# Seven products for the first image's keys, earlier loads, and a gate chain and norms that sit elsewhere

## The chip, the cores and the metric

The kernel runs on one core of a Trainium2 chip. The metric is the device time in microseconds (us) of one execution; the time of a kernel is the median of several runs. A profiled execution gives, beside its own time, a span: from its first to its last instruction.

## The reference

The input x is [4, 512, 32, 32]: four images of 512 channels and 1024 tokens. Four layers each add something to x, computed from a group norm of x (32 groups of 16 channels):

```
x = x + L0(gn(x)); x = x + L1(gn(x)); x = x + L2(gn(x)); x = x + L3(gn(x))

L0: q, k, v = w_q xf, w_k xf, w_v xf            # 8 heads of 64
    attn = softmax(w_head mixed over heads (q^T k * scale))
    attn = instance norm over (q, T) of each head; out = (attn v) w_proj^T + b_proj
L1: y = mean of x over the tokens; two layers of RY rotations and CNOTs on 9 qubits,
    q_out = expectations; x * sigmoid(q_out fc_w^T + fc_b)
L2: softmax attention, 8 heads of 64, with Wq, Wkv, Wp
L3: softmax over the 8 best of 2048 memory rows, their weighted sum
```

Everything is float32.

## The kernel before

`fast_net` (line 42) writes the whole order of work out by hand: Python generators are advanced at chosen places, and instructions that go through `pin` (line 56) keep their program order on their engine.

Start. `first` (305) loads x and w_q of image 0, normalizes, and makes q. `circuit` (815) prepares constants: the loads of whp (824, 32 small DMAs on SP), wmix (828), angles, their sine and cosine (854, on ACT), the matrices `turn` of the circuit, turned by fourteen calls of `rotate` (804: three DVE instructions each, lines 807, 808, 811), parities on POOL, and the `signs` (896 to 900). Then `take_k` (452) makes k of image 0 by `project` (193): four blocks of eight matmuls of 128x512 each, copied out by DVE (457). A matmul of float32 appears as two records on PE.

Layer 0 runs image by image in 32 steps of 32 queries (loop at 1721, `step` at 1611). In step s, `scores` (499) makes the scores of step s (510) in PSUM pairs, ACT copies them to ss (516), and eight DMAs, four issued by SP and four by POOL, relay them to s2 (525) so that heads lie side by side; `mix` (532) of step s-2 mixes heads by wmix (536), ACT takes the exponentials (543), DVE turns them (549) and takes their statistics (564), and `apply` (566, line 575) multiplies with v of step s-7. `sums` (583) and `scale` (637) normalize on POOL. In steps 0 to 6 `take_v` (461) makes v in bank pt. After step 31 seven steps follow without scores, in the first four of which q of the next image is made (`take_q`).

Around that, each step advances side work: `mid` (1689) advances `prepare` (423, the norm of the next image) in steps 9 to 12, 24, 28, 30 and 31, and one link of `state["behind"]`; `early` (1684) issues loads from a plan between the two halves of a step's scores. For the next image the plan of `next_image` (270) loads halves of a quarter of x (256 KB, 2 KB rows) in steps 20, 22, 24 and 26, two each in steps 28 and 29, and the four columns of w_q (256 KB, 512 B rows) in steps 30 to 33; they go through ACT's queue (`beside`, 266). For images 1 to 3 `collect` (655) loads further pieces in steps 7 to 18.

k of images 1 to 3 is made by `seven_keys` (1134): `seven` (1086) forms the 2x2 block product from seven products instead of eight (line 1112), each of four matmuls in one PSUM pair, which ACT copies (1145, where a block begins) or DVE adds (1041) to the block. `sums_k` (1116) makes their input sums on DVE: four sets ahead of the products, three more between them. In image 3's tail, k and v of layer 2 are made in the same way (`seven_by_channels` 1242, `seven_v` 1255).

The gate of layer 1 (`gating`, 904) is a chain of about sixteen links for each image, advanced by `next(state["behind"])`: two group averages (152, 162) and their small steps on POOL; `turned(0)` (929) and its rotation on POOL (922 to 926); `turned(1)` (934, 935) and its rotation; pr (939); the products of signs (944); zr (950, 955); the gate's product (959); exponential on ACT (967), reciprocal on DVE (971), and nine steps on POOL (975 to 983). All small products go to bank pt through `small_ps` (60). The chain advances in each of the seven closing steps of an image, then once after each of the seven products, and the rest in the next image's first steps. For `by_scalar` (after layer 0) the small copies run on ACT.

Layer 2 walks units of four key blocks (`scores2` 1340, `apply2` 1381). Between images a border makes q, k and v by seven products each (loops from 1874); `finish2` (1444, line 1452) scales a finished unit on DVE, which frees its PSUM bank; `small_ps` (1809) takes that bank at the border. `norm3` (1477) of the image before, or the gate of image 3 at the first border, is advanced once after each product. In image 0 of layer 2 the sums of the weights for the others are made by `weight_sums` (1055): Wq's from step 10, one per step.

Of the kernel before, what the change touches and what calls it, by code (L numbers as in the profile page):

```python
# [41 lines left out]
def fast_net(ctx: ExitStack, tc: tile.TileContext, a: dict, out: bass.AP, flag: bass.AP):  # L42
# [227 lines left out]
    def next_image(b, key, src):  # L270

        def half(k, n):
            def load():
                I = img[b]
                I["xn"] = xn_all
                beside(xn_all[:, k, n * NB:(n + 1) * NB], src[:, k, n * NB:(n + 1) * NB])
            return load

        halves = [half(k, n) for k in range(KC) for n in range(T // NB)]
        plan = {NEXT - 8 + 2 * i: halves[i:i + 1] for i in range(4)}  # L280
        plan |= {NEXT + i: halves[4 + 2 * i:6 + 2 * i] for i in range(2)}
        plan |= {NEXT + 2 + m: [load_columns(b, key, a[key], m)] for m in range(KC)}
        return plan
# [14 lines left out]
    def run_out(gen):  # L298
        for _ in gen:
            pass  # L300
# [514 lines left out]
    def circuit():  # L815
# [6 lines left out]
        for i in range(P // NH):  # L822
# [3 lines left out]
        m = from_ident(ident.rearrange("p (r q h) -> p q r h", r=4, q=4), AX.XY)  # L826
        pin(nc.vector.tensor_scalar_mul(m, m, SCALE))
        pin(nc.vector.tensor_mul(
            wmix.rearrange("p (g q) -> p g q", q=4),
# [23 lines left out]
        pin(nc.vector.tensor_scalar(ang, ang, lim, -lim, ALU.min, ALU.max))  # L853
        nc.scalar.activation(sincos, ang, AF.Sin)

# [18 lines left out]
        assert NP - 1 == 6  # L874
        for i in range(NP):
            for l, m in ((0, turn[:, 0:1]), (1, turn[:, 1:3])):
                rotate(
                    m.rearrange("p m (hi t lo) -> p (m hi) t lo", t=2, lo=HD >> i),
                    tmp[:, 1, 0:m.shape[1]].rearrange(
                        "p m (hi t lo) -> p (m hi) t lo", t=2, lo=HD >> i),  # L880
                    l * NQ + 2 + i,
                )


        par = e[:, 1].rearrange("p r qq k -> p (r qq k)").rearrange("p (i q) -> p i q", q=P)
        pin(nc.gpsimd.memset(par[:, 0], 1.0))
        for i in range(NP):
# [5 lines left out]
            pin(nc.gpsimd.tensor_scalar_mul(new_v[:, :, 1], old_v[:, :, 1], -1.0))  # L893
        pin(nc.gpsimd.tensor_mul(par, par, ident.rearrange("p f -> p () f").to_broadcast([P, NH, P])))
        own = const.tile([P, NH], F32, tag="own", name="own")
        pin(nc.vector.tensor_reduce(own, par, AX.X, ALU.add))
# [7 lines left out]
    def gating(b):  # L904
# [7 lines left out]
        def turned(l, products):  # L912
# [17 lines left out]
            ps[:, 0:KC], turn[:, 0], y, start=True, stop=True)))  # L930
        yield

        def second(ps):
# [151 lines left out]

    def seven(b, key, src, multiply, view, block, begin, done=None, own=None, put=None):

# [7 lines left out]
        for i, (at, uses) in enumerate(SEVEN):  # L1095
            ps = next_pair()
            multiply(ps, *factors[at])
            for *ij, op in uses:
                if put:
                    put(op, *ij, ps)  # L1100
                elif op == "=":
                    begin(*ij, ps)
                else:
                    (add7 if op == "+" else sub7)(block(*ij), block(*ij), view(ps))
            if done and i in LAST7:
                done(*LAST7[i][1])
            yield
# [25 lines left out]

    def seven_keys(b):

# [3 lines left out]
        def put(op, i, j, ps):  # L1139
            for m in range(2):  # L1140
# [5 lines left out]
                else:  # L1146
# [3 lines left out]
        return seven(b, "w_k", I["xn"], by_channels, None, None, None,  # L1150
                     own=I.pop("own7")(), put=put)

# [88 lines left out]

    def seven_by_channels(b, name, bias):

        dst = img[b][name] = big(name, f"{name}2_{b}")

        def begin(i, j, ps):
            for m in range(2 * i, 2 * i + 2):
# [4 lines left out]
        return seven(b, "W" + name, img[b]["xn"], by_channels, lambda ps: ps,  # L1252
                     lambda i, j: dst[:, 2 * i:2 * i + 2, j * NB:(j + 1) * NB], begin)

    def seven_v(b):

# [9 lines left out]

        return seven(b, "Wv", img[b]["xn"], by_tokens, by_head, block, begin)

# [334 lines left out]

    first()
    circuit()
    for m in range(KC):
        take_k(0, m, m + 1)

# [73 lines left out]
    state = {"behind": iter(())}  # L1682

    def early(b, s):

# [35 lines left out]
    for b in range(B):  # L1721
# [18 lines left out]
        for s in range(STEPS, STEPS + LAG):  # L1740
            step(b, s, lambda b, s: next(state["behind"], None),
                 lambda b, s: qs[s - STEPS](s + 1) if s < STEPS + KC else None)
# [18 lines left out]
        if last:  # L1761
# [3 lines left out]
            ring[:] = [1, 2, 0]  # L1765
            for i, _ in enumerate(seven_by_channels(0, "k", bk2)):
                next(state["behind"], None)
                if i < 3:
# [7 lines left out]
            run_out(norm)  # L1776
        for m, _ in enumerate(() if last else seven_keys(b + 1)):
            next(state["behind"], None)
            next(key_sums, None)
# [8 lines left out]
        if last:  # L1788
# [4 lines left out]
            sums7 = output_sums(b)  # L1793
            for i, _ in enumerate(seven_v(0)):
                if i < 2:
# [41 lines left out]
    for b in range(B):  # L1837
# [6 lines left out]
        for s, u in enumerate(UNITS2):  # L1844
# [6 lines left out]
            for _ in range(2):  # L1851
                if s >= 3 and last:
                    next(behind, None)
                if s >= 7:
                    next(ahead, None)
            if s == 9 and b == 0:
                weights = weight_sums(1, "Wq")
            if s >= 10 and b == 0:
                next(weights, None)
# [16 lines left out]
        for i, _ in enumerate(seven_by_channels(b + 1, "q", bq2)):  # L1876
# [4 lines left out]
            if i == 5 and b == 0:  # L1881
                run_out(weight_sums(1, "Wk"))
            next(behind, None)
        load_sums(b, "Wp", b == 0)
# [773 lines left out]
```

## Time and profile before

| what | value |
|---|---|
| median of 3 runs | 2538.16 us |
| lowest, highest | 2535.89, 2540.12 us |
| the profiled execution's own time | 2539.05 us |
| its span | 2537.3 us |
| mean granted TensorE clock | 0.996 |
| busy: PE, DVE, POOL, ACT | 2482.0, 1803.6, 1217.8, 1019.2 us |
| image 0: first exponentials of step 0 start at | 91.94 us |
| image 1, 2, 3: the same | 355.6, 646.3, 936.0 us |

Lines of the profile give the start, the length, the engine, the line of the kernel, the operation, out<-in, shapes and the count of merged instructions; in brackets stands the idle time of the engine before it and what ended it. PE is the tensor engine's matmul, PEld its weight load, DVE the vector engine, ACT the scalar engine, POOL GpSimd, SP the sync engine; a q behind an engine's name is its queue of issues. Some matmul records are missing from a trace.

### The profile page before, as it was taken

To read this page: it belongs to the slowest core of one execution; us is meant where nothing else is said; L and a number is where in the kernel's file an instruction comes from. 1 tells how busy PE (TensorE), PEld (TensorE's weight loads), DVE (VectorE), ACT (ScalarE), POOL (GpSimd) and SP (SyncE) were. 2 spreads that over 40 slices of the span, in tenths; PEclk is the share of its full clock that TensorE was granted. 3 is DMA by queue.
4 is the path that set the end of the run, shared out by engine and by line. 5 is a ranking of instruction groups with operands and counts; after the bars stand their busy time and mean duration, and the time that the engine had idled before them with its cause. 6 is when DMAs were issued, how large, how long until landed. Compare 5 with 4: busy or idle time off the path is not lost.

```text
span 2537.3 us, 48070 instructions
## 1 busy us (share of the span) xinstructions
PE 2482.0 (98%) x18520; PEld 1177.2 (46%) x18520; DVE 1803.6 (71%) x2940; ACT 1019.2 (40%) x1237; POOL 1217.8 (48%) x1688
## 2 busy tenths in 40 slices
PE   9999999999999999999999999999999999999998
PEld 4344534554355534545633633453363344444445
DVE  4599568875688548885768777576857648787876
ACT  1467346651665336651254145225314612121211
POOL 2266425553355525553185147117405616666665
PEclk9999999999999999999999999999999999999999
DMA  2578548872698528893211330131114046767666
GB/s 84 146 205 236 132 126 222 240 219 73 175 238 235 145 73 210 241 246 136 76 47 54 116 128 18 63 104 51 44 44 150 18 141 180 222 182 222 181 189 176
DMA packets 190031, 367.19 MB, mean 145 GB/s; under 512 B 32985, under 2 KB 96473, under 8 KB 185570
## 3 DMA queue, kind: packets, MB, share of 16 engines
q1 hardware_dynamic: 109712, 186.58, 23.7%
q0 software_dynamic: 49152, 142.79, 20.6%
q10 hardware_dynamic: 30930, 34.66, 5.1%
q8 instruction: 149, 2.44, 0.4%
q14 instruction: 88, 0.72, 0.1%
HBM read 190.10 MB, written 39.58 MB: 91 GB/s over the span
## 4 chain that ended last, share of the span: by engine, by line
PE 65%; issue 10%; POOL 10%; DVE 7%; DMA 5%; ACT 2%; SPq 0%; POOLq 0%; ACTq 0%; DVEq 0%
PE pair L1112 11%; PE pair L1358 7%; PE pv L575 7%; PE pair L199 7%; POOL got L1535 7%; PE pair L510 6%; PE pair L536 5%; PE pt L468 5%; PE pair L1238 4%; PE pt L1395 4%; PE pt L764 3%; PE pv L1395 3%; DMA s<-ss 2%; ACT e L543 2%; DVE eT L1377 1%
## 5 line engine op out<-in xcount | busy, mean ns | idle before, releaser
L549 DVE STREAM_TRANSPOSE eT<-e 128x1024 f32<-128x1024 f32 x256 | 316.6, 1237 | 203.3 <-ACT e L543 202.7
L525 POOL DMA_DIRECT2D s<-ss x512 | 258.0, 511 | 393.9 <-PE pair L536 128.5
L1535 POOL DMA_INDIRECT got<-in_mem,ix x256 | 279.7, 1093 | 214.2 <-DVE tmx L1541 142.0
L1352 ACT ACTIVATE eT<-pair 128x1024 f32<-128x1024 f32 x256 | 248.2, 1022 | 319.9 <-PE pair L1358 158.0
L564 DVE BATCH_NORM_STATS2 st<-e 128x6 f32<-128x256 f32 x1024 | 350.7, 404 | 0.0
L1376 POOL TENSOR_TENSOR e<-eT 128x1024 f32<-128x1024 f32 x96 | 240.4, 2507 | 166.8 <-ACT eT L1352 122.3
L543 ACT ACTIVATE e<-pair 128x1024 f32<-128x1024 f32 x256 | 250.5, 1022 | 164.3 <-PE pair L536 134.2
L516 ACT COPY ss<-pair 128x1024 f32<-128x1024 f32 x256 | 247.3, 1019 | 86.1 <-DMA s<-ss 44.0
L510 PE MATMUL pair<-k,q 64*32 64x512 f32 x4096 | 268.1, 600 | 12.8 <-ACT e L543 12.8
L575 PE MATMUL pv<-eT,v 128*64 128x128 f32 x4096 | 250.7, 276 | 4.0 <-ACT pv L635 4.0
L575 PEld LDWEIGHTS pv<-eT,v 128*64 128x64 f32 x4096 | 221.1, 137 | 71.7 <-issue 55.2
L1358 PE MATMUL pair<-q,k 64*128 64x512 f32 x1024 | 240.0, 605 | 2.0 <-DVE sum L1041 0.9
L1377 DVE TENSOR_TENSOR eT<-eT,e 128x1024 f32<-128x1024 f32 x96 | 142.5, 1485 | 129.4 <-POOL e L1376 129.2
L1372 POOL TENSOR_TENSOR eT<-eT 128x1024 f32<-128x1024 f32 x32 | 83.4, 2606 | 201.3 <-ACT eT L1352 197.4
L536 PE MATMUL pair<-s,wmix 32*32 32x512 f32 x4096 | 160.9, 602 | 6.9 <-DMA s<-ss 5.4
L1582 DVE SCALAR_TENSOR_TENSOR acc<-got,et,acc 128x512 f32<-128x512 f32 x210 | 157.9, 752 | 7.5
L1358 PEld LDWEIGHTS pair<-q,k 64*128 64x128 f32 x1024 | 92.2, 186 | 140.4 <-issue 66.4
L1515 ACT COPY att<-pair 128x1024 f32<-128x1024 f32 (+1 forms) x65 | 64.9, 999 | 221.2 <-PE pair L1510 212.4
L510 PEld LDWEIGHTS pair<-k,q 64*32 64x32 f32 x4096 | 57.2, 105 | 181.0 <-ACT e L543 86.9
L1041 DVE TENSOR_TENSOR k<-k,pair 128x512 f32<-128x512 f32 (+1 forms) x80 | 67.9, 893 | 78.3 <-PE pair L1112 62.1
L1530 DVE MAX8 top<-att 128x8 f32<-128x2048 f32 x31 | 71.1, 2293 | 73.0 <-issue 40.8
L1510 PE MATMUL pair<-memT,xn_d 128*128 128x512 f32 x256 | 120.7, 594 | 0.0
(380 smaller groups left out, 3737.5 us busy)
## 6 DMA issues: line engine op xcount, KB each, us to landing
s<-ss SPq DMA_DIRECT2D x512, 128.0 KB
s<-ss POOLq DMA_DIRECT2D x512, 128.0 KB
rb<-r POOLq DMA_DIRECT2D x64, 128.0 KB
o<-o SPq DMA_DIRECT2D x32, 256.0 KB
xr_c<-x SPq DMA_DIRECT2D x32, 256.0 KB
rb_c<-r SPq DMA_DIRECT2D x64, 128.0 KB
eT<-x SPq DMA_DIRECT2D x32, 256.0 KB
out<-eT SPq DMA_DIRECT2D x32, 256.0 KB
```

The source lines that it names most:

```text
L510: pin(nc.tensor.matmul(sc[m * NS:(m + 1) * NS, r, :], q[r * HD:(r + 1) * HD, m, s * NS:(s + 1) * NS], k_[r * HD:(r + 1) * HD, m, n * NB:(n ...
L516: pin(nc.scalar.copy(ss[:, :, n * NB:(n + 1) * NB], sc))
L525: pin(relays[side].dma_start(out=s2[2 * m + r::NH], in_=ss[m * NS:(m + 1) * NS, r, :]))
L536: pin(nc.tensor.matmul(mixed(s, r // 2)[t * NS:(t + 1) * NS, r % 2, :].rearrange("p (qq k) -> p qq k", qq=2), wmix[r * NS:(r + 1) * NS], s ...
L543: pin(nc.scalar.activation(e[:, half].rearrange("p r qq k -> p (r qq k)"), flat2(mixed(s, half)), AF.Exp))
L549: pin(nc.vector.transpose(eT[:, j % 2].rearrange("p b (qq i r) x -> p i r qq b x", qq=2, i=4)[:, i, 2 * half:2 * half + 2], e[:, half].rea ...
L564: pin(nc.vector.bn_stats(st[:, i, 2 * half + r, qq, :], e[:, half, r, qq, :]))
L575: pin(nc.tensor.matmul(pv[r * HD:(r + 1) * HD, gp, :], I["v"][:, t, g * HD:(g + 1) * HD], eT[:, j % 2, t, :, 4 * g:4 * g + 4], start=(t == ...
L1112: pin(nc.tensor.matmul(ps[:, m, :], w[:, k, m * P:(m + 1) * P], x[:, k, :], start=(k == 0), stop=(k == 1)))
L1352: pin(nc.scalar.activation(e, scs[len(es)], AF.Exp, scale=SCALE))
L1358: pin(nc.tensor.matmul(sc[:, r, :], I["k"][r * HD:(r + 1) * HD, m, t * P:(t + 1) * P], I["q"][r * HD:(r + 1) * HD, m, n * NB:(n + 1) * NB] ...
L1535: pin(nc.gpsimd.indirect_dma_start(out=got[:, i, :], out_offset=None, in_=a["mem"], in_offset=bass.IndirectOffsetOnAxis(ap=ix[:, i:i + 1], ...
```

## The change

Five edits in `fast_net`; the order of other work is as before.

1. `circuit` becomes a generator with yields ahead of wmix, ahead of and after the sine, and after each rotation; the parities on POOL stand ahead of the rotations. k of image 0 is made by `sums_k` and `seven_keys`: `circuit` is taken to wmix, four sets of sums are made, then wmix and the angles, then the seven products, with one set of sums and one stage of `circuit` after each. From the second product on that stage is one rotation; nine rotations and the signs follow at the end.
2. The plan for image 1's loads has one load in each of steps 8 to 19: eight halves, then four columns of w_q.
3. `gating` has one link more for images 0 to 2. The chain is advanced in four of the seven closing steps, no longer in the last three, and in the seven products through `between`, which runs after a product's matmuls and ahead of its evacuation (before: after it). What is left follows in the next image's steps 0 to 5, or in v's seven products after image 3.
4. At the borders of layer 2, the chain is advanced after products 2, 3, 5 and 6 of q (counted from 0) and not after the other three.
5. The sums of Wq in layer 2's image 0 begin in step 8 instead of 10.

In the built program PE's rows differ only in k of image 0 and in the places of the small products: L959 stands behind the v product of step 0 (images 2 and 3), and in image 3's tail the norm's product (694) stands directly behind the second L944.

```diff
@@ next_image
         halves = [half(k, n) for k in range(KC) for n in range(T // NB)]
+        if b == 1:
+            columns = [load_columns(b, key, a[key], m) for m in range(KC)]
+            return {TC + i: [load] for i, load in enumerate(halves + columns)}
@@ circuit
         pin(nc.vector.tensor_scalar_mul(m, m, SCALE))
+        yield
         pin(nc.vector.tensor_mul(
             wmix.rearrange("p (g q) -> p g q", q=4),
...
-        nc.scalar.activation(sincos, ang, AF.Sin)
+        yield
+        pin(nc.scalar.activation(sincos, ang, AF.Sin))
+        yield
...
-        for i in range(NP):
-            for l, m in ((0, turn[:, 0:1]), (1, turn[:, 1:3])):
-                rotate(
...
         pin(nc.gpsimd.tensor_mul(par, par, ident.rearrange("p f -> p () f").to_broadcast([P, NH, P])))
+        for i in range(NP):
+            for l, m in ((0, turn[:, 0:1]), (1, turn[:, 1:3])):
+                rotate(
...
+                yield
@@ gating
         yield
+        if not by_scalar:
+            yield
 
         def second(ps):
@@ seven (and the parameter between of seven_keys, seven_by_channels, seven_v)
             multiply(ps, *factors[at])
+            if between:
+                between()
             for *ij, op in uses:
@@ start
     first()
-    circuit()
-    for m in range(KC):
-        take_k(0, m, m + 1)
+    constants = circuit()
+    next(constants)
+    key_sums = sums_k(0)
+    run_some(key_sums, 4)
+    next(constants)
+    for i, _ in enumerate(seven_keys(0)):
+        next(key_sums, None)
+        next(constants)
+    run_out(constants)
@@ layer 0
+    def go_on():
+        next(state["behind"], None)
...
-            step(b, s, lambda b, s: next(state["behind"], None),
+            step(b, s, lambda b, s: go_on() if s < STEPS + KC else None,
...
-            for i, _ in enumerate(seven_by_channels(0, "k", bk2)):
-                next(state["behind"], None)
+            for i, _ in enumerate(seven_by_channels(0, "k", bk2, go_on)):
...
-        for m, _ in enumerate(() if last else seven_keys(b + 1)):
-            next(state["behind"], None)
+        for m, _ in enumerate(() if last else seven_keys(b + 1, go_on)):
...
-            for i, _ in enumerate(seven_v(0)):
+            for i, _ in enumerate(seven_v(0, go_on)):
@@ layer 2
-            if s == 9 and b == 0:
+            if s == 7 and b == 0:
                 weights = weight_sums(1, "Wq")
-            if s >= 10 and b == 0:
+            if s >= 8 and b == 0:
                 next(weights, None)
...
-            next(behind, None)
+            if i in (2, 3, 5, 6):
+                next(behind, None)
         load_sums(b, "Wp", b == 0)
```

More of the change, by code (lines that the diff above doesn't have):

```diff
@@ L874, in circuit @@
         assert NP - 1 == 6
-        for i in range(NP):
-            for l, m in ((0, turn[:, 0:1]), (1, turn[:, 1:3])):
-                rotate(
[L878 to L882, printed above, removed]
         par = e[:, 1].rearrange("p r qq k -> p (r qq k)").rearrange("p (i q) -> p i q", q=P)
@@ L894, in circuit @@
         pin(nc.gpsimd.tensor_mul(par, par, ident.rearrange("p f -> p () f").to_broadcast([P, NH, P])))
+        for i in range(NP):
+            for l, m in ((0, turn[:, 0:1]), (1, turn[:, 1:3])):
+                rotate(
+                    m.rearrange("p m (hi t lo) -> p (m hi) t lo", t=2, lo=HD >> i),
+                    tmp[:, 1, 0:m.shape[1]].rearrange(
+                        "p m (hi t lo) -> p (m hi) t lo", t=2, lo=HD >> i),
+                    l * NQ + 2 + i,
+                )
+                yield
         own = const.tile([P, NH], F32, tag="own", name="own")
@@ L1084, in by_head, with seven @@
         return ps.rearrange("p n (t c) -> p (n t) c", c=H)
-    def seven(b, key, src, multiply, view, block, begin, done=None, own=None, put=None):
+    def seven(b, key, src, multiply, view, block, begin, done=None, own=None, put=None, between=None):
         a11, s2, s5, a22 = quarters(img[b][key], H)
@@ L1132, in sums_k, with seven_keys @@
             yield
-    def seven_keys(b):
+    def seven_keys(b, between=None):
         I = img[b]
@@ L1150, in seven_keys @@
         return seven(b, "w_k", I["xn"], by_channels, None, None, None,
-                     own=I.pop("own7")(), put=put)
+                     own=I.pop("own7")(), put=put, between=between)
     def by_channels_of(ps, w, x):
@@ L1240, in by_tokens, with seven_by_channels @@
                     start=(k == 0), stop=(k == 1)))
-    def seven_by_channels(b, name, bias):
+    def seven_by_channels(b, name, bias, between=None):
         dst = img[b][name] = big(name, f"{name}2_{b}")
@@ L1252, in seven_by_channels, with seven_v @@
         return seven(b, "W" + name, img[b]["xn"], by_channels, lambda ps: ps,
-                     lambda i, j: dst[:, 2 * i:2 * i + 2, j * NB:(j + 1) * NB], begin)
-    def seven_v(b):
+                     lambda i, j: dst[:, 2 * i:2 * i + 2, j * NB:(j + 1) * NB], begin,
+                     between=between)
+    def seven_v(b, between=None):
         dst = img[b]["v"] = big("v", f"v2_{b}").rearrange("p k (i c) -> p (k i) c", c=C)
@@ L1265, in begin @@
                 bv2[:, i * H:(i + 1) * H].rearrange("p c -> p () c").to_broadcast([P, 4, H])))
-        return seven(b, "Wv", img[b]["xn"], by_tokens, by_head, block, begin)
+        return seven(b, "Wv", img[b]["xn"], by_tokens, by_head, block, begin,
+                     between=between)
     def seven_out(b):
```

## The prediction

> **What bounds the kernel now.** I read the page first: its busy line, then the waits of the tensor engine over the span, then the time order around each large wait, then tables by stretch with the granted clock and the DMA share.
>
> ```profile
> PE 2482.0 (98%) x18520; PEld 1177.2 (46%) x18520; DVE 1803.6 (71%) x2940; ACT 1019.2 (40%) x1237; POOL 1217.8 (48%) x1688
> ```
>
> PE has an instruction in flight for 2482 of 2537 us. So a change can shorten this kernel in three ways: fewer matmuls, smaller gaps in the 55 us, or no slow clock. The waits of PE (total, times, longest) name the gaps:
>
> ```profile
> PE pair L536 <- DMA s<-ss: 5.4, 4, 2.4
> PE pt L934 <- POOL amp L926: 5.4, 3, 2.5
> PE pt L152 <- DVE eT L1452: 5.0, 2, 2.6
> PE pt L944 <- POOL pr L939: 1.9, 2, 1.0
> PE pt L929 <- DVE ri L602: 1.4, 1, 1.4
> ```
>
> Three of the five are the gate's chain (L929, L934, L944); L152 is the norm at the borders of layer 2; L536 is mix waiting for the relayed scores. The time order at the end of image 3 shows what such a gap costs beyond itself:
>
> ```profile
> 1179.95 0.38 PE L934 MATMUL pt<-amp,turn 128*128 128x2 f32 x2 [2.49 <-POOL amp L926]
> ...
> 1180.42 5.38 PE L1112 MATMUL pair<-eT 128*128 128x512 f32 x8
> 1185.63 3.60 PE L1112 MATMUL pair<-eT,Wk_n 128*128 128x512 f32 x8
> ```
>
> The first of the seven products takes 5.38 us, the next, of the same shape, 3.60. The table by stretch (length, busy of PE, PEld, DVE, ACT, POOL, then granted clock, DMA share, GB/s) has the reason, and it is the same after the gaps near 257, 595 and 885 us:
>
> ```profile
> 256.00:266.00 10.00, 8.30 (x128) 2.98 (x128) 5.72 (x13) 7.29 (x8) 5.64 (x14) 0.83 1.04 235
> 594.00:604.00 10.00, 8.55 (x25) 3.83 (x22) 1.56 (x3) 2.64 (x5) 8.72 (x27) 0.83 0.16 54
> 884.00:894.00 10.00, 8.53 (x19) 3.99 (x20) 1.55 (x3) 2.64 (x5) 8.81 (x26) 0.83 0.09 29
> 1178.00:1188.00 10.00, 8.05 (x18) 3.78 (x19) 1.47 (x3) 2.48 (x5) 9.30 (x29) 0.83 0.49 158
> 1600.00:1610.00 10.00, 8.36 (x23) 4.06 (x24) 5.42 (x7) 3.85 (x8) 0.60 (x3) 1.00 0.24 80
> ```
>
> A mean clock of 0.83 over 10 us is 3.4 us at half speed: 1.7 us of work lost. It follows four of the gaps that the change touches; the gap at 1601 has none.
>
> [...] loads issued by ACT drive the DMA share to 1.04, and the relays of SP and POOL come late (the 2.4 us above). [...] DVE sits 14.13 us before wmix (L828) until the DMA of whp lands.
>
> **Part 1, k of image 0.**
>
> ```profile
> 41.79 27.63 PE L199 MATMUL pair<-xn_all,w_k 128*128 128x512 f32 x64
> 69.25 3.60 PE L468 MATMUL pt<-w_v,xn_all 128*128 128x512 f32 x8
> ```
>
> Before: 64 records in 69.25 - 41.79 = 27.46 us, 0.429 us each. Seven products of 8 records are 56: 24.03 us. Removed: 3.43 us of PE, if DVE keeps up. The sums: four sets ahead of wmix are 3 of 1024 elements (1.22 us) and 3 of 512 (0.69), 5.7 us, put ahead of the instruction that waits until 39.0, in DVE's idle 14.13 us; they end near 31, the first product starts at 41.8. Then products end at 45.2, 48.7, 52.1, 55.5, 59.0, 62.4, 65.8. DVE from 48.7: two adds into k 1.28 (the row at 605.12), sums 0.69 + 0.78 + 1.22, one rotation 0.9, two adds 1.3, sum 1.2, rotation 1.1, four adds 2.4, rotation 0.9, four adds, rotation, two, rotation, two: with each waiting for its product, the last add ends near 67.6. The v product in between covers it until 65.8 + 3.5 = 69.3, where the scores begin (before: 72.78). So 3.4 us, with 1.7 us of cover. If the cover goes, I lose what DVE is late: bounds 1.5 to 3.4. The nine rotations left (before: all fourteen in 13 us at 41.8 to 54.9), own and the signs then end near 77.5; DVE's next work, bn_stats at 84.68, lies behind that even 3.4 us earlier. ACT copies four blocks (0.58 each), loads the Sin table (1.28) and has two products' time before its pair is due. Nothing else is queued behind Sin but the k copies.
>
> **Part 2, loads of image 1, one per step 8 to 19** instead of 20 to 33 (with two in steps 28 and 29). Removed: the wait at 257 (2.4) and its slow clock (1.7): 4.1. Added, where steps are 5.5 us long:
>
> ```profile
> 131.00:198.00 67.00, 63.02 (x1144) 29.00 (x1132) 61.78 (x132) 46.83 (x51) 46.33 (x97) 1.00 0.78 209
> 198.00:242.00 44.00, 41.77 (x762) 19.14 (x758) 40.71 (x85) 31.91 (x35) 30.75 (x62) 1.00 0.86 236
> 242.00:276.00 34.00, 31.21 (x423) 14.79 (x435) 25.38 (x55) 19.68 (x21) 19.79 (x37) 0.95 1.04 230
> ```
>
> Twelve loads of 256 KB are 3.15 MB in 67 us: 47 GB/s on 209 is 256, a share of 0.78 x 256/209 = 0.96. That is under the ceiling (282 GB/s at share 1.01 in 210 to 220), yet close. Images 1 and 2 load one piece per step in their steps 7 to 12 and pay one mix wait there, 1.0 and 1.5 us (426, 717). Bounds: 0, and three waits of 1.5 with two slow clocks, 8. I take 2.5. ACT's issues (0.33 to 0.55 us) are the same number; xn and w2 are free by step 8 (v's last product is in step 6).
>
> **Part 3, the gate's chain of images 0 to 2.** It pauses in the last three steps, goes on ahead of the evacuations of the seven products, and the extra link puts two products (6.9 us) between the first rotation and L934. Rotating takes POOL 2 to 4 us (591.7 to 595.7), now behind the last scale, which thereby starts earlier. L944 follows its pr by one to two products; u's copy on DVE sits behind two adds, a sum and bn_stats, so I see pr some 2 us ahead of L944. Gains: image 1 1.45 + 0.97 + 1.7 = 4.1; image 2 the same 4.1; image 3 1.43 + 2.49 + 1.7 = 5.6. Added: in the two image changes the gate's product (L959) now stands right behind the v product of step 0 and shares its bank pt; ACT's copy of v takes 0.59 us from 0.11 after the product's end, so PE waits 0.8 each. Behind L959 wait the scores of step 1. In image 3 the norm's product now follows L944 on pt and waits for DVE's copy of zr: an estimate of 0.6 from the 0.15 us copy and DVE's lag. Net 3.3 + 3.3 + 5.0 = 11.6; bounds 4 to 14. POOL's 9 closing steps of 0.2 us come in step 5, ahead of a relay; steps there last 7.1 us, and the relays have more than a step in hand.
>
> **Part 4, later norms at the borders.** L152 at the first product waits 2.65 and 2.33 us for L1452 to free its bank; L1452 ends at 1601.6, and two products later (1606) nothing is left to wait for. 5.0 us, bounds 3 to 5. At the first border there was no such wait. The sums of Wq two steps earlier fall into DVE's idle stretches at 1320 to 1327 (2.6 and 4.0 us) and leave the crowded 1341 to 1369, where PE waited 1.05 (L1395) and 0.70 (L1112): I take 0.9, bounds -1 and 1.75. Wq's DMA stores pass one group of r and rb on SP: 0.3 us of issue, nothing.
>
> **Sum.** 3.4 + 4.1 - 2.5 + 11.6 + 5.0 + 0.9 = 22.5 us. Against the profiled execution's own 2539.05 us (span 2537.30 and 1.75 around it): 2516.5. That execution lies 0.9 above the median 2538.16, so on the median 2515.7, say 2516.
>
> **Rivals.** (a) As worked out, 2516, 2510 to 2522: chance 0.60. (b) The chain waits in its new places: DVE takes u late behind its adds, POOL's pr is late at L944; 2.5 us and a slow clock in three images give back 12.6: 2528, 0.13. For it: u's copy is behind some 4 us of DVE work; against: DVE had idle time there (7.14 us ahead of 605.12). (c) The loads cost their upper bound, 5.5 more: 2522, to 2526: 0.12. (d) Both: 2534, no measurable change, 0.05. (e) Slower: the twelve loads saturate DMA. If every step from 8 to 19 loses what the step at 257 lost, 2.4 us, with a slow clock in every second, that is 12 x 2.4 + 6 x 1.7 = 39 against 25 gained: 2552. It decides from 25/12 = 2.1 us a step. The share 0.96 speaks against it: 0.05. (f) Better than 2510, as waits of ACT and DVE shrink too: 0.05.
>
> **Numbers.** Faster by over 0.2% (5 us, about what a measurement of this kernel can tell from no change) are a, b, c, f: 0.90; same d: 0.05; slower e: 0.05. The range 2509 to 2526 holds a, c, most of f and part of b.
>
> **What would show it.** Right: 56 records in 24 us, scores at 69.3; no clock of 0.83 near 257, 592, 878 and 1165; no waits at L934, L944, L929, and L152; new waits of 0.8 at L959. PE's busy time falls by 3.4 + 4 x 1.7 = 10 us. Wrong: waits of L510 or L536 on k or DMA between 66 and 200 us, a wait at L944 on pr, or steps of 6 us or more where they had 5.5.

## The result and the profile after

The changed kernel takes 2519.56 us (median of 6 runs, 2519.18 to 2524.26), the kernel before 2537.02 us beside it (6 runs, 2533.37 to 2540.12). The ratio is 0.9936, 95% interval 0.9924 to 0.9949: 17.5 us faster. The forecast was 2516 with a range of 2509 to 2526. The profiled execution's own time is 2519.18 us and its span 2517.5, which is 19.8 below the span before.

Line numbers after the change are higher by 3 in layer 0's steps (mix is L539), by 5 to 9 in the gate and in the sevens (`turned(0)` L934, `turned(1)` L941 and L942, signs L951, gate's product L966, the sevens L1121, their sums L1048) and by 11 in layer 2.

The page's busy line of the kernel after:

```profile
PE 2474.3 (98%) x18512; PEld 1174.9 (47%) x18512; DVE 1822.0 (72%) x2962; ACT 1022.8 (41%) x1245; POOL 1224.0 (49%) x1688
```

PE's busy time falls by 7.7 us where I had 10. The rest of the gain is gaps. The waits of PE over the span (total, times, longest):

```profile
...
PE pair L539 <- DMA s<-ss: 3.3, 5, 1.1
PE pair L1437 <- DVE s_c L1423: 2.5, 1, 2.5
...
PE pt L1406 <- DVE eT L1463: 2.2, 1, 2.2
...
PE pt L966 <- ACT v L475: 1.5, 2, 0.8
PE pt L941 <- POOL amp L931: 1.1, 1, 1.1
...
PE pt L697 <- DVE zr L137: 0.3, 1, 0.3
```

Gone are L934, L951 and L152 of the kernel after (929, 944 and 152 before). One wait of the second rotation, L941, is left at 1.1 us. L966 and L697 are the new waits that part 3 forecast at 0.8 and 0.6 us. L1437 is new, L1406 has grown from 1.05 us (L1395 before), and nothing in the forecast has either: both lie in layer 2's image 0, near 1338 and 1340 us.

The table by stretch (length, busy of PE, PEld, DVE, ACT, POOL, granted clock, DMA share, GB/s) at the places that had a slow clock, and at the new waits:

```profile
248.00:258.00 10.00, 9.79 (x184) 4.68 (x176) 9.28 (x20) 7.98 (x9) 7.65 (x14) 1.00 0.78 199
588.00:598.00 10.00, 10.00 (x43) 5.05 (x38) 3.16 (x6) 2.88 (x6) 8.54 (x20) 1.00 0.35 99
873.00:883.00 10.00, 10.00 (x57) 5.52 (x53) 3.18 (x6) 2.64 (x5) 8.45 (x17) 1.00 0.22 70
1172.00:1182.00 10.00, 8.93 (x25) 4.00 (x24) 8.71 (x11) 1.26 (x2) 8.01 (x19) 1.00 0.68 236
1336.00:1346.00 10.00, 5.67 (x22) 1.76 (x22) 7.76 (x12) 2.23 (x3) 3.35 (x2) 0.83 0.32 132
```

All four slow clocks are gone, and there is one where none was. k of image 0 in the time order of PE:

```profile
41.24 3.60 PE L1121 MATMUL pair<-sk,sk 128*128 128x512 f32 x8
44.67 7.03 PE L1121 MATMUL pair<-sk,w_k 128*128 128x512 f32 x16
51.54 7.03 PE L1121 MATMUL pair<-xn_all,w_k 128*128 128x512 f32 x16
58.40 3.60 PE L1121 MATMUL pair<-sk,sk 128*128 128x512 f32 x8
61.84 3.60 PE L1121 MATMUL pair<-sk 128*128 128x512 f32 x8
65.27 3.60 PE L471 MATMUL pt<-w_v,xn_all 128*128 128x512 f32 x8
68.80 1.52 PE L513 MATMUL pair<-k,q 64*32 64x512 f32 x24
```

8 + 16 + 16 + 8 + 8 = 56 records in 65.27 - 41.24 = 24.03 us, with no gap. By segments of the span, from starts of marked instructions (us; "image" runs from the first to the last exponentials of an image, "change" from there to the next image's first, "tail" to layer 2's first scores):

| segment | before | after | difference | forecast |
|---|---|---|---|---|
| first k product to image 0 | 50.15 | 46.71 | -3.44 | -3.4 |
| image 0 of layer 0 | 194.97 | 195.74 | +0.77 | -1.6 |
| changes to images 2 and 3 | 151.61 | 143.83 | -7.78 | -6.6 |
| tail of image 3 | 104.53 | 100.27 | -4.26 | -5.0 |
| image 0 of layer 2, to the first border | 112.01 | 117.45 | +5.44 | -0.9 with the next |
| first border | 84.60 | 83.49 | -1.11 | |
| second and third border | 167.46 | 161.94 | -5.52 | -5.0 |
| sum of these | | | -15.9 | -22.5 |

The remaining 3.9 us of the 19.8 lie in segments that no part was to change: the start (-0.55), images 1 and 3 (-1.6 and -1.1) and the last layer (-0.6). Across the kernels below, image 1 took 212.7 to 214.1 us with and without the change's parts, so that share is scatter of this pair of profiles. Two terms have the wrong sign: the sums of Wq (+4.3, not -0.9) and, on the average of the profiles below, the loads.

### The profile page after: what moved, and what is told of

The parts are those of the page before. It is cut to its first block, busy times and chain, and to the rows that moved or that the text cites. A ratio compares the mean times of both kernels' runs of the same rounds, so it can differ in the third digit from the quotient of the medians.

```text
span 2517.5 us, 48084 instructions
## 1 busy us (share of the span) xinstructions
PE 2474.3 (98%) x18512; PEld 1174.9 (47%) x18512; DVE 1822.0 (72%) x2962; ACT 1022.8 (41%) x1245; POOL 1224.0 (49%) x1688
## 4 chain that ended last, share of the span: by engine, by line
PE 87%; DMA 4%; DVE 3%; ACT 2%; issue 1%; POOL 1%; SPq 0%; ACTq 0%; POOLq 0%
PE pair L1521 17%; PE pair L1121 12%; PE pair L1369 8%; PE pv L578 8%; PE pair L513 6%; PE pair L199 6%; PE pair L539 6%; PE pt L471 5%; PE pt L1406 4%; PE pv L1406 4%; PE pair L1247 4%; PE pt L767 4%; DMA s<-ss 3%; ACT e L546 2%; DVE out L1048 1%
## 5 line engine op out<-in xcount | busy, mean ns | idle before, releaser
L539 PE MATMUL pair<-s,wmix 32*32 32x512 f32 x4096 | 162.7, 599 | 3.4 <-DMA s<-ss 3.3
L1048 DVE TENSOR_TENSOR k<-k,pair 128x512 f32<-128x512 f32 (+1 forms) x96 | 78.1, 857 | 65.8 <-PE pair L1121 52.1
L651 POOL TENSOR_TENSOR o<-pv,rb 64x256 f32<-64x256 f32 x128 | 118.8, 928 | 6.3
```

What stands on the lines that cost most here:

```text
L539: pin(nc.tensor.matmul(mixed(s, r // 2)[t * NS:(t + 1) * NS, r % 2, :].rearrange("p (qq k) -> p qq k", qq=2), wmix[r * NS:(r + 1) * NS], s ...
```

## The experiments

Theory from this profile: the earlier sums of Wq make DVE late in layer 2's image 0, which is the 4.3 us; the loads cost more, and gain less, than the forecast had; the rest works as forecast. Each kernel is the changed kernel with one edit, except where said. "Image 0" is layer 0's unless layer 2 is named.

### Sums of Wq as before (e1)

```diff
-            if s == 7 and b == 0:
+            if s == 9 and b == 0:
                 weights = weight_sums(1, "Wq")
-            if s >= 8 and b == 0:
+            if s >= 10 and b == 0:
```

> The changed kernel with the sums of Wq in layer 2's image 0 begun in step 10 again, as before. Theory: starting them in step 8 puts them into the same two steps as the four normalizations of the next image on DVE, and that made PE wait 2.5 us for the key sums (L1437), 2.2 us for finish2 (L1463) and run 3.4 us at half clock; undone, image 0 of layer 2 (first score of layer 2 to its border) takes 112.0 us again instead of 117.4, and the first border 84.6 instead of 83.5: about 4.3 us less in all, 2515. Rival: those waits were an accident of the one profiled execution; then the time stays within 1 us of 2519.5.

Measured: 2512.99 us (2511.83 to 2517.21), ratio to before 0.9895 (0.9876 to 0.9914). Layer 2's image 0 is back at 112.01 us and the first border at 84.60, the wait of L1437 is gone, that of L1406 is 1.1, and the clock is 1.00 there. By segments that is 4.3 us, by medians 6.6. So this part of the change is a loss, and its undoing beats the changed kernel (the two intervals don't overlap).

Why it loses is in the time order of DVE in the changed kernel:

```profile
1319.56 0.68 DVE L1048 TENSOR_TENSOR sums<-Wq 128x512 f32<-128x512 f32 x1
...
1321.89 3.59 DVE L1025 TENSOR_SCALAR xn_c<-xn_c,sa,ta 128x1024 f32<-128x1024 f32 x2
1325.40 2.84 DVE L1048 TENSOR_TENSOR Wq<-Wq 128x512 f32<-128x512 f32 x1
1328.17 3.38 DVE L1388 TENSOR_TENSOR eT<-eT,e 128x1024 f32<-128x1024 f32 x1
...
1336.70 1.24 DVE L1423 TENSOR_REDUCE s_c<-est 128x16 f32<-128x512 f32 x2
```

and of POOL beside it:

```profile
1322.12 5.57 POOL L1387 TENSOR_TENSOR e<-eT 128x1024 f32<-128x1024 f32 x2 [2.74 <-DVE eT L1388]
1327.94 2.52 POOL L1383 TENSOR_TENSOR eT<-eT 128x1024 f32<-128x1024 f32 x1 [0.25 <-ACT eT L1363]
```

A sum of this size takes 0.68 us at 1319.56; the one at 1325.40 takes 2.84 and ends 0.55 after POOL's products do (1327.69). The product at 1328.17 takes 3.38 where others take 1.22, and ends 1.09 after POOL's next instruction (1330.46). DVE then reaches s_c (L1423), which PE waits for, at 1337.94. In these two views POOL's instruction starts 0.50 and 0.23 us before DVE's (1324.90, 1327.94), and DVE's ends only after it. Why DVE's takes longer there, the traces don't show. In the kernel with late sums POOL's two products stand apart, at 1319.65 to 1322.46 and from 1323.23, and the sum at 1322.93 slips between them in 0.68 us (its DVE, then its POOL):

```profile
1322.93 0.68 DVE L1048 TENSOR_TENSOR eT<-Wq 128x512 f32<-128x512 f32 x1
1323.53 3.37 DVE L1388 TENSOR_TENSOR eT<-eT,e 128x1024 f32<-128x1024 f32 x1
```

```profile
1319.65 2.81 POOL L1387 TENSOR_TENSOR e<-eT 128x1024 f32<-128x1024 f32 x1 [1.40 <-DVE eT L1388]
1323.23 2.58 POOL L1387 TENSOR_TENSOR e<-eT 128x1024 f32<-128x1024 f32 x1 [0.78 <-ACT eT L1363]
```

In the changed kernel POOL's two products stand back to back, since the first had to wait 2.74 us for DVE, and there is no such space. The long product is no cost of the change: it takes 3.37 us with late sums too. The sum's 2.84 is new.

The loss adds up: new waits 2.48 + 2.25, less the 1.05 that stood at the second place before, plus 1.7 for 3.41 us at half clock (granted clock 0.50 from 1340.90 to 1344.31 us), is 5.4 us, as the segment has it.

### Which of the sums (e5, e9)

First two steps of pause after the third sum (steps 8, 9, 10, then 13 on):

```diff
-            if s >= 8 and b == 0:
+            if s in (8, 9, 10, 13, 14, 15) and b == 0:
```

> The changed kernel with the five sums of Wq in steps 8, 9, 10, 13 and 14 of layer 2's image 0 (the closing stores in 15): begun as early as in the change, but not in steps 11 and 12, where the four normalizations of the next image are. Theory: only the two sums in steps 11 and 12 do harm, since DVE is full there; then there are no waits of over 1.1 us at L1437, L1406 and no slow clock, and image 0 of layer 2 takes 112 us: as with the late start, 4.3 us under the changed kernel. Rival: it is the early start as such, through the stores of the sums or DVE work in steps 8 to 10; then waits stay and the stretch takes 115 us or more.

Measured: 2517.6 us (2513.51 to 2518.22), ratio 0.9918 (0.9892 to 0.9944); layer 2's image 0 takes 116.72 us. PE's time order in this kernel:

```profile
1337.82 0.31 PE L1437 MATMUL pair<-s_c,same 128*64 128x32 f32 x4 [2.49 <-DVE s_c L1423]
1339.77 5.22 PE L1406 MATMUL pt<-eT,v 128*64 128x512 f32 x16 [1.64 <-DVE eT L1463]
```

The first wait is whole, the second shorter by 0.6, and the product after it still runs partly at the slow clock (0.83 from 1336 to 1346 us; it takes 5.22 us, where 16 records take 3.65). I had put the normalizations one step too late; the trace has them in steps 10 and 11, so the sum of step 10 was still among them, and it took 2.84 us again. The next kernel leaves steps 10 and 11 free:

```diff
-            if s >= 8 and b == 0:
+            if s in (8, 9, 12, 13, 14, 15) and b == 0:
```

> The changed kernel with the sums of Wq in steps 8, 9, 12, 13 and 14 of layer 2's image 0 (and what follows them in step 15): none in steps 10 and 11, where the next image's normalizations run on DVE beside POOL. Theory: the sum in step 10, which takes 2.84 us where others take 0.69, is what makes DVE late; then the waits near 1338 and 1340 (2.48 and 2.25 us) are gone or at most 1.1 us, no half clock follows, image 0 of layer 2 takes 112 to 113 us and the whole some 5 us less than the changed kernel, 2513 to 2515. Rival: the start in steps 8 and 9 is itself the cost, since it uses up DVE's slack ahead of the normalizations; then that image stays at 116 us or more, as it did when the third sum was left in step 10.

Measured: 2516.34 us (2513.74 to 2520.28), ratio 0.9919 (0.9891 to 0.9947). Layer 2's image 0 takes 112.11 us and the first border 84.60. DVE and PE in this kernel:

```profile
1322.97 3.58 DVE L1025 TENSOR_SCALAR xn_c<-xn_c,sa,ta 128x1024 f32<-128x1024 f32 x2
1326.47 3.37 DVE L1388 TENSOR_TENSOR eT<-eT,e 128x1024 f32<-128x1024 f32 x1
```

```profile
1336.60 0.31 PE L1437 MATMUL pair<-s_c,same 128*64 128x32 f32 x4
1338.08 3.65 PE L1406 MATMUL pt<-eT,v 128*64 128x512 f32 x16 [1.17 <-DVE eT L1463]
```

The sums of steps 8 and 9 stay early, and PE doesn't wait for them; without the sum of step 10 the wait for s_c is gone. That is the theory, and the rival, that the early start alone makes PE wait, falls. But the loss takes both. The early start uses up DVE's slack (the 1.72 us for which DVE stands idle before 1318 us in e1 are gone here too), and only behind it does the sum of step 10 meet POOL: in e1 the first sum stands in step 10 and takes 0.68 us. The wait of 1.17 us is close to what it was before the change (1.05). All fourteen kernels agree: the eight with sums in steps 8, 9 and 10 have the slow clock once between 1336 and 1346 us and take 116.7 to 118.4 us for this image; the six others, with the sums from step 10 on or with none in steps 10 and 11, have no slow clock there and take 112.0 to 112.1. The median lies above the 2513 to 2515 expected, but its gain of 3.2 us can't be told from 5.

### The plan of image 1's loads (e2, e3, e10, e12)

The old plan with all else changed:

```diff
-        if b == 1:
-            columns = [load_columns(b, key, a[key], m) for m in range(KC)]
-            return {TC + i: [load] for i, load in enumerate(halves + columns)}
```

> The changed kernel with the plan of loads of before (steps 20 to 33). Theory: the loads of one per step cost 4.9 us in steps 11 to 19 and saved 4.1 us, so moving them was worth nothing; image 0 (first exponentials of step 0 to those of step 31) takes 195 us, as in both kernels, and the time stays within 2 us of 2519.5. In steps 11 to 19 the distances go back to 6.04, 6.26, 5.34, 5.71, and the mix wait of over 2 us near step 29 with its slow clock comes back. Rival, my prediction: the move is worth 1.6 us net, so the old plan gives 2521 or more, with image 0 at 196.5.

Measured: 2517.49 us (2516.74 to 2519.68), ratio 0.9913 (0.9894 to 0.9932); image 0 takes 193.79 us. The late wait is back with 1.37 us instead of over 2, and without a slow clock. So no gain from moving the loads shows: by the medians it costs 2.1 us, with intervals that overlap. The tables by stretch, first of the changed kernel, then of this one:

```profile
127.00:200.00 73.00, 67.33 (x1164) 30.54 (x1154) 63.08 (x134) 46.99 (x51) 47.34 (x98) 1.00 0.95 239
200.00:242.00 42.00, 39.77 (x733) 17.70 (x735) 38.68 (x80) 31.16 (x35) 28.78 (x58) 1.00 0.74 211
242.00:276.00 34.00, 33.09 (x486) 17.07 (x471) 27.51 (x58) 22.37 (x24) 23.28 (x45) 1.00 0.78 216
```

```profile
127.00:200.00 73.00, 68.81 (x1258) 32.15 (x1256) 68.06 (x146) 50.28 (x54) 49.43 (x103) 1.00 0.79 212
...
242.00:276.00 34.00, 31.60 (x438) 15.16 (x407) 25.18 (x52) 21.19 (x22) 20.47 (x40) 1.00 0.96 252
```

The share of 0.95 in the loaded steps is what the forecast worked out (0.96), and it isn't free: 1164 records of PE in 73 us instead of 1258. What the loads delay is the relays. The waits of all engines in that stretch of the changed kernel begin with

```profile
ACT ss L519 <- DMA s<-ss: 14.0, 7, 3.1
```

ACT can't copy new scores to ss while the relay still reads the old ones (3.3 us in five waits in the kernel before). PE shows only part of it as idle: mix takes 2.14 us at 150.09 where its 32 records otherwise take 1.14, a wait inside the group.

For all kernels I took the distances between the first exponentials of neighbouring steps of image 0, and the shortest of each over all kernels but the last (e12); these add up to 189.6 us. Time above that, in steps 7 to 19 and from step 20 on:

| kernel | steps 7 to 19 | from 20 | image 0 |
|---|---|---|---|
| before, old plan (e2), keys only (e4) | 1.1, 1.6, 1.3 | 4.3, 2.6, 1.7 | 195.0, 193.8, 192.6 |
| changed, e1, e5, e6, e7, e9, e11 (one load per step) | 6.0, 5.3, 4.1, 4.3, 6.8, 5.9, 5.7 | 0.1 to 0.2 | 194.1 to 196.8, mean 195.5 |
| every second step (e3, e8) | 2.0, 2.0 | 1.6, 2.8 | 193.2, 194.3 |
| columns alone early (e12) | 1.1 | 4.0 | 194.8 |
| no halves (e10) | 0.8 | 1.6 | 192.0 |

One load per step costs 5.4 on average in the early steps against 1.3 with the old plan, and saves what is a draw: 4.3 in the profile that the forecast rests on, 2.6 and 1.7 in the two others. The net is 195.5 - 193.8 = +1.7 us, not -1.6. It is a mean of seven profiles against one of three, and the two ranges overlap (194.1 to 196.8, 192.6 to 195.0): a loss is likely, and its size is rough.

Halves in every second step, columns in steps 24 to 27:

```diff
-            return {TC + i: [load] for i, load in enumerate(halves + columns)}
+            return ({TC + 2 * i: [load] for i, load in enumerate(halves)}
+                    | {NEXT - 4 + i: [load] for i, load in enumerate(columns)})
```

> The changed kernel with image 1's halves loaded in every second step, 8, 10 to 22, and the four columns of w_q in steps 24 to 27. Theory: what costs is the DMA share of 0.95 for twelve steps on end; with a load in every second step the relays have time to catch up, neither the 4.9 us of steps 11 to 19 nor the wait near step 29 appear, and image 0 takes 191 us instead of 195.7: 2515. Rival: the columns with their 512 B rows are what delays the relays; then the wait moves to steps 26 to 29 and image 0 takes 194 us or more.

Measured: 2518.28 us (2515.06 to 2524.09), ratio 0.9922 (0.9897 to 0.9947). Image 0 takes 193.18 us, 2.6 less than in the changed kernel's profile and between the 191 of the theory and the 194 of the rival; the early steps lose 2.0 instead of 6.0, but 1.6 comes back from step 20 on. The medians can't show it (their runs scatter by 9 us).

The halves left out, columns one per step from step 30 as before:

```diff
-            columns = [load_columns(b, key, a[key], m) for m in range(KC)]
-            return {TC + i: [load] for i, load in enumerate(halves + columns)}
+            img[b]["xn"] = xn_all
+            return {NEXT + 2 + m: [load_columns(b, key, a[key], m)] for m in range(KC)}
```

> The changed kernel without the eight loads of image 1's x in image 0 (they are left out: image 1's normalized input is made from what image 0 left in that buffer); the four columns of w_q are loaded one per step from step 30, as in the kernel before. Theory: the halves are the whole cost of the loads; then image 0 takes 190.5 to 191 us from its first to its last exponentials, which is the sum of undisturbed step distances, and no step from 8 to 19 exceeds it by over 0.1 us. Against the changed kernel (195.7 in its profile) that is 5 us. Rival: the relays and the columns cost something alone; then that stretch takes 192 us or more.

Measured: 2515.57 us (2513.6 to 2518.31), ratio 0.9919 (0.9891 to 0.9946). The steps from 9 to 19 are within 0.1 us of the shortest: the loads in steps 8 to 19 are the cost there, and since columns alone in four of these steps add nothing (e12 below: 1.1 us, the old plan 1.3), it is mainly the halves. But image 0 takes 192.0 us, as the rival had it, since one late step is 1.4 us too long:

```profile
258.91 2.20 PE L539 MATMUL pair<-s,wmix 32*32 32x512 f32 x32 [0.43 <-issue]
```

mix takes 2.20 instead of 1.14 us, with 0.43 before it, although no half of x was loaded. One column had been issued at 250.62, the relays at 254.09 and 255.82. So the wait near 257 isn't the halves' alone. The last kernel asks whether it is the columns' alone; it stands on the kernel of the last section (2511.0 us), with the halves in their old places:

```diff
-        if b == 1:
-            columns = [load_columns(b, key, a[key], m) for m in range(KC)]
-            return {TC + 2 * i: [load] for i, load in enumerate(halves + columns)}
...
-        plan |= {NEXT + 2 + m: [load_columns(b, key, a[key], m)] for m in range(KC)}
+        at = TC if b == 1 else NEXT + 2
+        far = 3 if b == 1 else 1
+        plan |= {at + far * m: [load_columns(b, key, a[key], m)] for m in range(KC)}
```

> As the kernel with the sums of Wq from step 10, one link more for image 2's gate and sparser loads (2511.0 us), but with another plan for image 1: its halves of x as in the kernel before (steps 20, 22, 24 and 26, two each in steps 28 and 29), and only the four columns of w_q early, in steps 8, 11, 14 and 17. Theory: the late wait near 257 us comes from the column in step 30, whose 512 B rows lie ahead of the relays that mix waits for (without any halves it was still there, 1.42 us); then no step from 20 on exceeds its undisturbed length by over 0.3 us, and image 0 takes 191 to 192 us from its first to its last exponentials, the whole 2508 to 2509.5 us. Rival: the two halves each of steps 28 and 29 are the cause, as the prediction had it; then a wait of 1.4 us or more stays near 257 and image 0 takes 192.5 us or more, with the whole at 2510 us or more.

Measured: 2514.78 us (2511.11 to 2517.24), ratio 0.9916 (0.9884 to 0.9948); image 0 takes 194.8 us. The theory falls, by the step near 257 us, by image 0 and by the whole:

```profile
255.19 2.12 PE L538 MATMUL pair<-s,wmix 32*32 32x512 f32 x32 [1.47 <-DMA s<-ss]
```

Halves in steps 28 and 29 give the wait without a column, and a column in step 30 gives it without a half; the seven kernels with no load from step 20 on don't have it. Those steps can't take either without a loss; steps 8 to 19 take one load in two for about 0.7 us (2.0 instead of 1.3). What makes the late steps so tight, with a DMA share of 0.84 from 242 to 276 us when the halves are left out, I didn't settle.

### The gate's chain (e6, e11)

The extra link taken out:

```diff
-        if not by_scalar:
-            yield
```

> The changed kernel without the additional link of the gate's chain. Theory: the rotations on POOL start behind the last scale and end 0.6 us after the third product in images 1 and 2 and 4.6 us after it in image 3's tail (600.2 against 599.6 and 1177.1 against 1172.5 in the changed kernel's profile), so L934 of the kernel before waits again: 0.7 us in each of the two image changes (71.9 becomes 72.6) and 4.6 us instead of 1.1 in the tail, with a slow clock (100.3 becomes 105): about 7 us in all, 2526. Rival: the place behind the scores alone, ahead of the evacuations, is what took the waits away; then the time stays at 2519.5.

Measured: 2524.38 us (2522.93 to 2525.43), ratio 0.9955 (0.9936 to 0.9974), 4.8 above the changed kernel. The tail takes 104.10 us instead of 100.27 and the two changes 72.45 each instead of 71.91, together 4.9 (7 expected: the tail's wait came back with 3.58 us, not 4.6). PE's time order in the tail, first of the changed kernel, then without the link:

```profile
1165.37 0.28 PE L934 MATMUL pt<-amp,turn 128*128 128x4 f32 x2
1165.51 7.11 PE L1121 MATMUL pair<-eT,Wk_n 128*128 128x512 f32 x16
1172.46 3.60 PE L1121 MATMUL pair<-xn_all,Wk_n 128*128 128x512 f32 x8
1177.13 0.38 PE L941 MATMUL pt<-amp,turn 128*128 128x2 f32 x2 [1.07 <-POOL amp L931]
```

```profile
1176.63 0.38 PE L939 MATMUL pt<-amp,turn 128*128 128x2 f32 x2 [3.58 <-POOL amp L931]
```

Three products stand between the rotations with the link (10.4 us; I had two, 6.9), and 1.07 us is still missing, since POOL does the last four scalings of image 3 (L651, 4.50 us) ahead of its rotation. Without the link two products stand there, PE waits 3.58, and the clock is 0.83 in the ten us after it. With 1.07 us it stays at 1.00 (1174 to 1184 us).

The chain advanced after the evacuations of each product, with link and pause kept:

```diff
-        for m, _ in enumerate(() if last else seven_keys(b + 1, go_on)):
+        for m, _ in enumerate(() if last else seven_keys(b + 1)):
+            go_on()
```

and the same at `seven_by_channels` and `seven_v`.

> The changed kernel with the gate's chain advanced after each product's evacuation, as before the change, and not between its matmuls and its evacuation; the extra link and the pause are kept. Theory: the copies of u and zr on DVE then queue behind up to four adds (some 2.4 us), so the product of signs waits about 1 us for pr in each image change: 73 us instead of 71.9, and image 3's tail takes some 101.5 instead of 100.3; in all 3 us slower than the changed kernel. Rival: the place ahead of the evacuations is worth nothing, since the extra link alone gives enough distance: 71.9 and 100.3 stay.

Measured: 2521.46 us (2517.54 to 2525.73), ratio 0.9942 (0.9926 to 0.9957), 1.9 above the changed kernel, with intervals that overlap; the segments show more. The change to image 2 takes 73.17 us and the tail 101.18, but the change to image 3 stays at 71.91: 2.2 us of the expected 3.

```profile
612.80 0.35 PE L951 MATMUL pt<-pr,signs 128*9 128x1 f32 x8 [1.19 <-POOL pr L946]
```

So the place ahead of the evacuations is worth about 1 us where DVE has adds queued. In the tail the link counts most (3.8 of 4.3 us); in each image change it gives 0.5 and the place 1.3 or nothing. What is left of the 3.9 I put down to the pause, which moves the first rotation behind the first product; that isn't shown, since the pause alone wasn't tried and each part was only taken out with the others in place.

### The norms at the borders (e7)

The chain advanced after each product of q again:

```diff
-            if i in (2, 3, 5, 6):
-                next(behind, None)
+            next(behind, None)
```

> The changed kernel with the chain advanced after each of the seven products of q at layer 2's borders, as before. Theory: the waits of L152 for the bank that finish2 frees come back at the second and third border (2.6 and 2.3 us), which take 83.9 and 83.6 us instead of 80.97: 5.5 us more, 2525. Rival: in the changed kernel something else already held these borders, then less than 2 us come back.

Measured: 2527.92 us (2524.11 to 2534.67, 17 runs), ratio 0.9973 (0.9962 to 0.9985). The second and third borders take 83.86 and 83.83 us instead of 80.97, 5.8 together, and the first 84.10 instead of 83.49. The wait is back:

```profile
1589.97 0.27 PE L152 MATMUL pt<-mv_d,gavg 128*128 128x4 f32 x1 [2.62 <-DVE eT L1463]
```

In the changed kernel the same product stands after the third, and nothing is in brackets:

```profile
1592.15 0.28 PE L152 MATMUL pt<-mv_d,gavg 128*128 128x4 f32 x2
```

The medians differ by 8.4 us; 6.4 of it are the borders. The other 2 us lie in places that this edit doesn't touch: in its profile image 0, image 3 and layer 2's image 0 took 1.1, 1.2 and 1.0 us longer than in the changed kernel's, and the start 1.1 less.

### Part 1 alone (e4)

The kernel before with k of image 0 by seven products and nothing else of the change (the edits of `circuit` and of the start).

> The kernel before with the new k of image 0 alone (circuit as a generator, four sets of sums, seven products). Theory: 8 records of 0.429 us fewer, all on the path: the first exponentials of image 0 start 3.4 us earlier relative to the first product, and the kernel takes 3.4 us less than before, 2533.6 for 2537.0. Rival: the 3.4 us are given back at the wait for the relays near step 29, which then starts earlier but ends with the same loads; then image 0 takes longer by as much and the time is that of before.

Measured: 2533.89 us (20 runs, 2529.44 to 2539.71), ratio 0.9987 (0.9977 to 0.9997), 2.8 us below before. From the first k product to image 0 it takes 46.71 us, as in every kernel with this part. Image 0 takes 192.6 us (195.0 before), so the rival, that image 0 gives the 3.4 us back, falls. The whole fits 3.4 us but is too rough to show it: its interval goes from 0.8 to 5.8 us.

### What the experiments point to (e8)

Sums of Wq from step 10 as before, one load in every second step from 8 to 30, and one link more for image 2's gate (that of the tail), so that the 1.07 us at L941 go:

```diff
-            return {TC + i: [load] for i, load in enumerate(halves + columns)}
+            return {TC + 2 * i: [load] for i, load in enumerate(halves + columns)}
...
+        if b == B - 2:
+            yield
...
-            if s == 7 and b == 0:
+            if s == 9 and b == 0:
...
-            if s >= 8 and b == 0:
+            if s >= 10 and b == 0:
```

> The changed kernel with three edits of its own: Wq's sums from step 10, image 1's twelve loads in every second step from 8 to 30, and one link more for the gate of image 2 (in image 3's tail, where L934 of before still waited 1.1 us). Theory: layer 2's image 0 112.0 and its border 84.6 us (4.3 less in all), image 0 at most 192.5 us (3 less: neither twelve loads on end nor four in two steps), the tail 99.2 (1.1 less): about 8.5 us under the changed kernel, 2511. Rival: the relays of the scores lose as much to twelve loads in any order, then image 0 stays at 193.2 or more and the time is 2513.5.

Measured: 2511.0 us (2508.28 to 2513.12), ratio 0.9894 (0.9868 to 0.992), the lowest median of all, 8.6 below the changed kernel, with no overlap of the intervals. From the kernel with late sums alone (e1, ratio 0.9895) it can't be told. The tail takes 98.56 us with no wait at L941, layer 2's image 0 112.02. The loads did less than hoped: image 0 takes 194.3 us, with a wait of 1.03 at 260.7 us.

## Why the prediction was right, and where not

The forecast held, with case (a) at 2516 against 2519.6, because three of its five parts were right and carried 20.0 of the 22.5 us, and the two wrong ones together (8.5 us worse than forecast) cost less than the range allowed for. A part of how close it came is luck: the terms as measured add up to 14.9 us, and the other 2.6 of the measured 17.5 belong to no term.

- **k of image 0**: -3.4 forecast, -3.44 measured. Products at 3.43 us, DVE never late: its last add into k ends at 66.76 (67.6 forecast), the signs at 76.8 (77.5).
- **Gate's chain**: -11.6 forecast, -12.0 measured. The image changes gave 3.9 each (3.3 forecast), the tail 4.3 (5.0), because L941 kept 1.07 us. The forecast didn't divide the gain among its three means; the extra link turned out to be worth 3.8 us in the tail and only 0.5 in an image change. The new waits were priced well: 0.77 twice for 0.8, 0.33 for 0.6. Rival (b), a late pr at L951, needs the advance after the evacuations to show, and then costs 1.2 us, not 2.5 with a slow clock in three images.
- **Borders**: -5.0 forecast, -5.5 measured, and 5.8 when undone.
- **Sums of Wq: the step that failed.** It said that they "fall into DVE's idle stretches at 1320 to 1327 (2.6 and 4.0 us)" and leave the crowded ones, for 0.9 with -1 as the worst. Layer 2 starts 17.9 us earlier after the change, so those stretches are at 1302 to 1309. Only the first sum (1305.62) lies there; the second and third stand at 1319.56 and 1325.40, around the normalizations, where DVE has no idle time: busy 13.97 of 14 us from 1318 to 1332. And a sum was priced at 0.69 us wherever it stands; the one that counts, beside POOL's products, took 2.84. At 0.68 it would have made DVE 2.2 us less late, which is most of the 2.48 that PE waits (an estimate from these lines). The cost is 4.3 net, outside the bound. Its small gain was real: the first border is 1.1 us shorter.
- **Loads: wrong sign on average, within its bounds.** The gain of 4.1 was read off one profile, whose wait near 257 us (2.38, with a slow clock) is a draw: the same plan gave 1.37 in one kernel and 0.4 in another, so 2.7 on average for the late steps. The cost was taken at 2.5; it is 4.1 (5.4 less the 1.3 that the old plan has in the same steps) and 0.3 more in the step ahead of them. So -1.6 should have been about +1.7. This net lies nearer to that of rival (c), +3.9, than to that of (a), and (e), saturation, is far off: its deciding price was 2.1 us a step, the mean is below 0.5. The 282 GB/s that it took for the ceiling at a share of 1.01 aren't one: from 2175 to 2185 us the kernel before moves 370 at the same share.
- **PE's busy time**: four slow clocks gone and one new give 3 x 1.7 + 3.4 = 8.5 against 7.7 measured; the forecast 10 had no new one.

With the measured terms the sum is -3.4 + 1.7 - 12.0 - 5.5 + 4.3 = -14.9, within the measured interval of 13 to 19 us.

## What to carry to other kernels

Place each moved instruction by what its neighbours are in the new order, step by step, and not by clock times of the old trace. Do it for every one of a series: here the first sum stood where it was forecast, and the third did the harm. Where POOL is busy, price a DVE instruction by the length that a trace shows for its kind beside POOL: here 2.84 us for a sum instead of 0.68. And a wait that comes and goes between runs is a mean to be estimated from several traces before its removal is counted as a gain.

## What the hardware showed that I had not expected

Beside POOL's products a DVE sum of 128x512 took 2.84 us instead of 0.68 and a product of 128x1024 took 3.38 instead of 1.22; two normalizations of 128x1024 took 3.59 beside POOL and 1.53 without (1337.86 us). By the ends these look like waits for POOL's instruction and not like a lower rate: the sum and the second of the two normalizations end 0.55 us after POOL's, the product 1.09. A run with POOL idle wasn't tried.

The slow clock (granted clock 0.50 for 3.41 us, in the changed kernel from 1340.90, in the kernel before four times) came after gaps of 2.48 and 2.25 us that lie within 5 us, and after a single one of 3.58 (e6). The length of a gap doesn't decide alone: the ten us after a gap of 2.05 before mix at 1113 us (kernel e11) have a clock of 0.83, those after 2.22 at 176 us (e9) and after 2.65 at 1601 us (before) have 1.00. Even 1.45 us at 595 and 1.47 at 885 (both before), with two small products next, had it.

The place of the gap explains most of this. The slow clocks of one trace start whole multiples of 3.413 us apart: in the kernel before at 259.10, 597.02, 887.15 and 1180.70 us, which is 99, 85 and 86 times. I cut each of the fourteen spans at such points, without its first 50 and last 20 us, and added up PE's idle time in each piece at full clock. All 13 pieces with 1.93 us or more are followed by the slow clock, and no piece with less than 1.45 is; between them 4 are, and others, up to 1.88, are not. The gap of 2.05 lies whole in one piece; that of 2.22 is cut into 0.83 and 1.39, that of 2.65 into 1.55 and 1.10. So some 2 us of idle time within one piece were enough in these traces: 2.02 in the piece from 255.69 and 2.49 in that from 1177.29 us (before), 2.85 in that from 1337.48 (changed kernel). What sets the length of the pieces, they don't show.
